# First layer: self_feat of six batches from seven half-size products, token sums on ScalarE, one load and some key products at other places

## The chip, the cores and the metric

The kernel runs on one core of one Trainium2 chip. The core has a matrix engine (TensorE, PE in the profile), a vector engine (VectorE, DVE), an engine for activation functions (ScalarE, ACT), a general engine (GpSimd, POOL) and one that here issues DMA transfers (SyncE, SP). Each works through its own list of instructions in order; semaphores make one wait for another. Matrix products land in PSUM, everything else lies in SBUF. GpSimd does not touch PSUM here.

The metric is the device time of one execution in microseconds, the median of the runs. The profile is one further execution, with the start and end of every instruction.

## The reference

Two layers run on x of shape (8, 512, 512): eight batches, 512 tokens, 512 features. All is float32. Cut to what matters:

```python
# layer 1: attention over the first NONGT = 20 tokens, edges as mask and bias
row_zero  = v.sum(-1) == 0
q_exp     = where(row_zero[..., None], 0, q[:, None, :])
self_feat = concat([v, q_exp], -1) @ W_self.T + b_self
output    = self_feat
for d in range(2):                       # the adjacency and its transpose
    A = (adj if d == 0 else swap(adj))[:, :, :20, :]       # int labels 0/1, last axis 11
    aff = q_heads(self_feat) . k_heads(self_feat[:, :20]) / sqrt(32)     # 16 heads
    aff = where(A.sum(-1) > 0, aff, NEG) + (A @ w_bias + b_bias)
    output += project(softmax(aff) @ self_feat[:, :20]) + bout
x = v + relu(output)

# layer 2: self attention with a layer norm conditioned on q, before and after
h   = gamma(q) * norm(x) + beta(q)
q, k, v = split(h @ Wqkv.T + bqkv)       # 16 heads
out = (softmax(q k^T) / sqrt(512)) @ v
h1  = out @ Wp.T + bp + x
y   = gamma(q) * norm(h1) + beta(q) + h1
```

The part that changes is `self_feat`. Its first 512 input features are x itself, so per batch it is a product of a 512 x 512 weight with a 512 x 512 input. The other 512 are the same condition vector for every live token, which the kernel adds as a bias times a row of ones (`LIVE`); a token whose features sum to zero gets no condition.

## The kernel before, in words

**Layout.** 128 partitions hold one slice of an axis at a time. `VT[b]` is batch b with features on partitions (four slices of 128 by 512 tokens), `ws` the weight, `SF[b]` the result with output features on partitions, `X[b]` the batch with tokens on partitions, `KQ[b]` the keys already multiplied into the query weights. Matrix products accumulate over the four slices.

**Blocks.** The first layer runs over 32 blocks, one per batch b and 128 tokens c (line 565); n is the number of the block, 4 b + c. Three chains of work overlap:

- two blocks ahead, `scores0` (L463): sixteen 320-column matmuls (L471), the query bias added by DVE (L475), then on POOL a multiplication with the mask (L477) and the addition of the edges (L481, in `add_edges`). `less_top` (L484) takes the maximum on DVE (L488) and subtracts it on POOL (L489).
- one block ahead, `normalize0` (L491): the exponential on ACT (L492), the sums and reciprocals on DVE (L495, L496), the division on POOL (L497).
- for the block itself, `turn_weights` (L499): five transposes on PE (L503) and their copy `wt` by ACT (L505), and `result0` (L508): transposes of `SF` (L513) and five matmuls (L515) into PSUM, added to x by DVE (L516), stored to `mid` by SP (L517).

**Work for later batches** lies in the same blocks. `self_feat` (L310) makes a quarter of a later batch's output features: four 512-column matmuls (L300), a bias row by ACT (L307), the addition by DVE (L308). Batch b + 1 gets its last two quarters in blocks c = 0 and 1, and batch b + 2 its first two in c = 2 and 3. `edges` (L242) turns a quarter of the labels into mask and addend, five instructions on DVE (L251 to L255); after the fourth quarter `far_away` (L257) adds the large negative numbers on POOL (L260, L261). At the end of c = 0, `live_sums` (L278) sums X[b + 2] over features on DVE (L281) and compares with zero (L283); in c = 1, `live_of` (L285) transposes that into a row of ones and zeros with PE (L289) and ACT (L291). Loads of X, VT, labels and the value weights for later batches are issued by SP at fixed blocks.

**Keys.** The products of keys and query weights for batches 4 to 7 are made in blocks 10 to 13 (`keys`, L407), half of each before `result0` and half at the end of the block, after the edges (L621). Blocks 15 to 18 also take layer norm statistics of batch 0 (L93), blocks 22 and 23 normalise it (L111).

**Order.** `manual_schedule` keeps the order in which the Python code issues instructions, engine by engine. What waits for what follows from the tiles. A pool with `bufs=4` hands out four buffers in turn; a fifth tile waits until the first one's readers are done. `bank` has four PSUM banks, `pair` two pairs of banks.

**The start.** SP issues the weights, VT of batch 0, `wc`, X of batch 0, `x_kv` (the first 20 tokens of all batches) and further weights. DVE sums `x_kv` (L347) for the condition of the near tokens (PE transposes, L355), and X of batch 0 in `live_sums(0)` (L349). `psk` (L325) occupies both PSUM pairs until DVE has moved it on (L363); the pair of `live_of(0)` comes after.

**The second layer** already makes its q, k, v and output projections of later batches from seven products of half the rows and columns (`product`, L709, matmuls at L719; sums of weights at L685 on DVE, of tokens at L693 on POOL). It is not touched but for a helper, `quarter`, that moves to the top.

Of the kernel before, what the change touches and what calls it, by code (L numbers as in the profile page):

```python
# [18 lines left out]
B, N, F = 8, 512, 512  # L19
P = 128  # L20
C = N // P
# [23 lines left out]
def graph_then_self_attention(ctx: ExitStack, tc: tile.TileContext, x, x_t, near, near_t, labels, w_self_t, wq, wk_t,  # L45
                              wout_t, wg_t, wb_t, wqkv_t, wp_t, cols, gate_vecs, rows, out):
    nc = tc.nc
# [111 lines left out]
    def value(c):  # L159
# [4 lines left out]
            nc.scalar.copy(V[0][:, c, :], out)  # L164
        return Group(f"pv1_0_{c}", lambda k: HT[0][:, k, c * P:(c + 1) * P], lambda k: W1[2][:, k, :], after)


    with ExitStack() as l0:
        w0 = l0.enter_context(tc.tile_pool(name="w0", bufs=1))
# [8 lines left out]
        def bank(name):  # L178
            return ps.tile([P, 512], F32, tag="bank", name=name)
# [34 lines left out]
        load_vt(0)  # L214
        wc = weight("wc", w_self_t[F:2 * F, :])
        x_kv = wring.tile([MH, 2, F], F32, tag="w", name="x_kv")
        load_x(0)
        nc.sync.dma_start(x_kv, near.rearrange("i m f -> m i f"))

        def room(name):  # L220
            return w0.tile([P, 3 * C * HM], F32, tag="kq3", name=name)
# [53 lines left out]

        LT = {}

        def live_sums(b):  # L278

            sums = two.tile([P, C, 1], F32, tag="sums", name=f"sums_{b}")  # L280
            nc.vector.tensor_reduce(sums, X[b], AX.X, ALU.add)  # L281
            LT[b] = two.tile([P, C], F32, tag="lt", name=f"lt_{b}")
            nc.vector.tensor_scalar(LT[b], sums.rearrange("p c o -> p (c o)"), 0.0, None, ALU.not_equal)  # L283

        def live_of(b):  # L285

# [23 lines left out]
        def self_feat(b, blocks_of_f):  # L310

            self_feat_rest(b, self_feat_main(b, blocks_of_f))

        def q_row(b):
            QR[b] = two.tile([P, HM], F32, tag="q_row", name=f"q_row_{b}")
# [249 lines left out]
        for n, (b, c) in enumerate(slots):  # L565
            turn_weights(b, c)

            if n + 3 == len(slots):
                scores0(*slots[n + 2])
            if n + 1 < len(slots):  # L570
                normalize0(*slots[n + 1])
            if n + 3 < len(slots):
                scores0(*slots[n + 2])
            if n + 2 < len(slots):
                add_edges(*slots[n + 2], nc.vector if n + 3 == len(slots) else nc.gpsimd)
            if b + 1 + c // 2 < B:
                self_feat(b + 1 + c // 2, ((c + 2) % 4,))
            if 26 <= n < len(slots) - 2:
                less_top(*slots[n + 2])
            if c == 1 and b + 2 < B:  # L580
                live_of(b + 2)
                if b + 3 < B:
                    load_vt(b + 3)
            if n in (10, 11, 12, 13):
                keys(1, n - 10, 0)
            if n in (24, 25):
                for f in (2 * (n - 24), 2 * (n - 24) + 1):
                    turn(0, f)
            group = {26: lambda: q_or_k(0, 0), 27: lambda: q_or_k(1, 0), 29: lambda: value(0), 30: lambda: value(1),
                     31: lambda: value(2)}.get(n, lambda: None)()  # L590
            if group:
                group.half(0)
                if n < 30:
                    group.half(1)
            if n == 10:
                gate_columns(gb)
            result0(b, c)
            if n >= 30:
                group.half(1)
            if n < 26:  # L600
                less_top(*slots[n + 2])
            if b + 1 + c // 2 < B:
                edges(b + 1 + c // 2, (c + 2) % 4)
            if c == 0 and b + 2 < B:
                live_sums(b + 2)
            if c == 1:
                if b + 1 < B:
                    far_away(b + 1)
                    load_vo(b + 1)
                if b + 2 < B:  # L610
                    load_labels(b + 2)
            if c == 2 and b + 2 < B:
# [51 lines left out]

    M = F // 2
    SUMS = {}

    def quarter(t, p, q):  # L670

        return t[:, 2 * p:2 * p + 2, M * q:M * (q + 1)]

    def a_(i, p, q):
        return quarter(W1[i], q, p)
# [458 lines left out]
```

## Time and profile before

| what | value |
|---|---|
| median of 3 runs | 1322.12 us (1321.79 to 1322.92) |
| profiled execution | 1322.61 us |
| its span, first to last instruction | 1320.8 us |
| mean granted TensorE clock | 0.999 |
| PE busy | 1303.7 us, 99% |
| DVE busy | 945.8 us, 72% |
| POOL busy | 811.3 us, 61% |
| ACT busy | 685.9 us, 52% |
| first transposes (L503) of block 0, block 26, block 31 | 77.51, 356.96, 398.43 us |

A row of a timeline gives start and length in us, engine, line and operation, the tiles written and read, the shape, and in brackets how long the engine had been idle and what ended that. The row of an engine in a list of waits gives the total in us, the count and the longest one. PE is shown twice, as matmuls (PE) and as weight loads (PEld). A float32 matmul or weight load appears as two records. Matmul records overlap[...]: eight records of four 512-column matmuls cover 3.60 us in all, while the last of them is 0.59 us long. So the distance between starts, and not the busy share, tells what a matmul costs.

### The profile page before, as it was taken

To read this page: it belongs to the slowest core of one execution; us is meant where nothing else is said; L and a number is where in the kernel's file an instruction comes from. 1 tells how busy PE (TensorE), PEld (TensorE's weight loads), DVE (VectorE), ACT (ScalarE), POOL (GpSimd) and SP (SyncE) were. 2 spreads that over 40 slices of the span, in tenths; PEclk is the share of its full clock that TensorE was granted. 3 is DMA by queue.
4 is the path that set the end of the run, shared out by engine and by line. 5 is a ranking of instruction groups with operands and counts; after the bars stand their busy time and mean duration, and the time that the engine had idled before them with its cause. 6 is when DMAs were issued, how large, how long until landed. Compare 5 with 4: busy or idle time off the path is not lost.

```text
span 1320.8 us, 29329 instructions
## 1 busy us (share of the span) xinstructions
PE 1303.7 (99%) x11203; PEld 959.1 (73%) x11203; DVE 945.8 (72%) x1721; ACT 685.9 (52%) x1670; POOL 811.3 (61%) x897
## 2 busy tenths in 40 slices
PE   9999999999999999999999999999999999999997
PEld 6566676666665687777777777777777777777776
DVE  4467776677746568687768768776785976776887
ACT  1322222222325666666665666666667567566664
POOL 0056554556563546677577667757866774775776
PEclk9999999999999999999999999999999999999999
DMA  9524552353212000001002000100200010010010
GB/s 337 185 88 138 173 192 74 104 168 127 90 66 72 1 2 1 1 18 65 2 2 81 2 2 17 66 2 1 81 1 1 18 65 1 1 50 2 10 42 33
DMA packets 46490, 78.64 MB, mean 60 GB/s; under 512 B 9680, under 2 KB 14224, under 8 KB 46352
## 3 DMA queue, kind: packets, MB, share of 16 engines
q1 hardware_dynamic: 45920, 76.22, 16.9%
q8 instruction: 90, 1.47, 0.5%
q10 hardware_dynamic: 432, 0.55, 0.1%
q14 instruction: 48, 0.39, 0.1%
HBM read 59.27 MB, written 17.49 MB: 58 GB/s over the span
## 4 chain that ended last, share of the span: by engine, by line
PE 87%; DVE 7%; POOL 2%; issue 1%; DMA 1%; ACT 1%; POOLq 0%; SPq 0%; DVEq 0%; ACTq 0%
PE pst L719 19%; PE pt L875 17%; PE s L850 10%; PE pss L471 9%; PE pao L890 8%; PE psf L300 6%; PE psp L762 6%; PE po L515 2%; PE pqk L138 2%; DVE top L857 2%; PE pz L124 1%; PE ptw L503 1%; PE pw L440 1%; PE pq L421 1%; PE pv L138 1%
## 5 line engine op out<-in xcount | busy, mean ns | idle before, releaser
L870 POOL TENSOR_SCALAR e<-e,den 128x512 f32<-128x512 f32 x511 | 366.8, 718 | 262.4 <-DVE den L867 168.3
L862 ACT ACTIVATE e<-s,top 128x512 f32<-128x512 f32 x512 | 348.9, 699 | 132.0 <-DVE top L857 128.7
L857 DVE TENSOR_REDUCE top<-s 128x2 f32<-128x1024 f32 x256 | 301.0, 1217 | 18.5 <-PE s L850 17.1
L875 PEld LDWEIGHTS pt<-ident,e 128*128 128x128 f32 x2048 | 234.5, 141 | 82.5 <-POOL e L870 25.9
L875 PE MATMUL pt<-ident,e 128*128 128x128 f32 x2048 | 289.7, 276 | 3.4 <-ACT et L877 1.6
L877 ACT COPY et<-pt 128x512 f32<-128x512 f32 x369 | 209.8, 597 | 100.6 <-PE pt L875 99.9
L471 PE MATMUL pss<-kq,sf 128*128 128x320 f32 x512 | 143.2, 433 | 1.0 <-DVE kq L428 1.0
L850 PE MATMUL s<-k_pair,q_pair 32*128 32x512 f32 x992 | 143.7, 640 | 0.0
L890 PEld LDWEIGHTS pao<-et,v 128*32 128x32 f32 x4096 | 107.5, 110 | 44.4 <-issue 44.4
L890 PE MATMUL pao<-et,v 128*32 128x128 f32 x4096 | 126.5, 274 | 0.0
L471 PEld LDWEIGHTS pss<-kq,sf 128*128 128x128 f32 x512 | 94.9, 190 | 37.5 <-ACT sf L307 1.5
L300 PE MATMUL psf<-vt,ws 128*128 128x512 f32 x256 | 115.0, 593 | 0.0
L862 ACT ACTIVATION_READ_ACCUMULATOR e<-s,top 128x1 f32 x512 | 109.4, 214 | 0.0
L877 DVE COPY et<-pt 128x512 f32<-128x512 f32 x143 | 96.3, 673 | 3.4 <-PE pt L875 2.8
L497 POOL TENSOR_TENSOR t<-t,den 128x640 f32<-128x640 f32 x32 | 40.7, 1273 | 81.3 <-DVE den L496 80.7
L300 PEld LDWEIGHTS psf<-vt,ws 128*128 128x128 f32 x256 | 48.3, 190 | 50.7 <-issue 46.6
L505 ACT COPY wt<-ptw 128x640 f32<-128x640 f32 x32 | 22.2, 693 | 104.3 <-PE ptw L503 104.2
L477 POOL TENSOR_TENSOR t<-t,mask 128x640 f32<-128x640 f32 x32 | 49.4, 1544 | 33.8 <-issue 30.2
L489 POOL TENSOR_TENSOR t<-t,top 128x640 f32<-128x640 f32 x32 | 40.7, 1273 | 38.4 <-DVE top L488 38.4
L492 ACT ACTIVATE t<-t 128x640 f32<-128x640 f32 x32 | 23.6, 738 | 77.6 <-POOL t L489 77.6
L126 ACT ACTIVATE ht<-pz,gates_t 128x512 f32<-128x512 f32 x32 | 24.7, 778 | 64.0 <-PE pz L124 64.0
L488 DVE TENSOR_REDUCE top<-t 128x32 f32<-128x640 f32 x32 | 26.2, 818 | 44.3 <-POOL t L481 44.2
(251 smaller groups left out, 2105.9 us busy)
## 6 DMA issues: line engine op xcount, KB each, us to landing
x<-in_x SPq DMA_DIRECT2D x8, 1024.0 KB
mid<-x SPq DMA_DIRECT2D x32, 256.0 KB
xq<-mid SPq DMA_DIRECT2D x8, 1024.0 KB
out<-o SPq DMA_DIRECT2D x31, 256.0 KB
vt<-in_x_t SPq DMA_DIRECT2D x7, 1024.0 KB
labels<-in_labels SPq DMA_DIRECT2D x16, 440.0 KB
wq<-in_wq SPq DMA_DIRECT2D x4, 1024.0 KB
gate<-gates SPq DMA_DIRECT2D x8, 512.0 KB
```

The source lines that it names most:

```text
L300: nc.tensor.matmul(psf[f], ws[:, k, f * P:(f + 1) * P], VT[b][:, k, :], start=(k == 0), stop=(k == C - 1))
L471: nc.tensor.matmul(o, SF[b][:, k, cut], KQ[b][:, k, on], start=(k == 0), stop=(k == C - 1))
L477: nc.gpsimd.tensor_tensor(t, t, MASK[b][:, c, None].to_broadcast([P, H, D2]), ALU.mult)
L719: nc.tensor.matmul(out[:, m, :], fixed[:, k, m * P:(m + 1) * P], moving[:, k, :], start=(k == 0), stop=(k == 1))
L762: nc.tensor.matmul(out[:, m, :], t[:, k, m * P:(m + 1) * P], a[:, k, :], start=(k == 0), stop=(k == 1))
L850: nc.tensor.matmul(S[n][j // 2][:, j % 2, :], Q[b, g][on, c * P:(c + 1) * P], K[b, g][on, :], start=True, stop=True)
L857: nc.vector.tensor_reduce(TOP[n][:, 2 * pair:2 * pair + 2], S[n][pair], AX.X, ALU.max, negate=True)
L862: nc.scalar.activation(e, S[n][pair][:, j % 2, :], AF.Exp, bias=TOP[n][:, j:j + 1], accum_out=DEN[n][:, j:j + 1])
L870: engine.tensor_scalar(E[n][j], E[n][j], DEN[n][:, j:j + 1], att_scale, ALU.mult, ALU.mult)
L875: nc.tensor.transpose(pt[:, k * P:(k + 1) * P], E[n][j][:, k * P:(k + 1) * P], ident)
L877: copy(et, pt.rearrange("p (k n) -> p k n", k=C))
L890: nc.tensor.matmul(PAO[b, g][DH * j:DH * (j + 1), at], V[b][:, k, DH * h:DH * (h + 1)], ET[n, j][:, k, :], start=(k == 0), stop=(k == C - 1))
```

## The change

**Seven products.** For batches 2 to 7, `self_feat` is made in the manner of the second layer: `ws`, `VT[b]` and `SF[b]` are each cut into four quarters (half of the partition slices, half of the columns), and seven products of quarters replace the sixteen full-width matmuls of a batch. One product is two times two matmuls of 256 columns. `weight_sums0` makes four sums of weight quarters once, on DVE, in blocks 0 and 1. `turned_sums` makes four differences of `VT` quarters per batch on POOL: two at the end of block c = 0, one in c = 1, one in c = 2. Products 1 and 2 of batch b + 2 run in c = 2, 6 and 7 in c = 3, then 4 and 5 in c = 0 of the next batch and 3 in c = 1. ACT copies product 1 and writes the four bias rows at once. DVE adds products 2 to 5 from PSUM to the result, and 6 and 7 to a running sum; the running sums (`TO_ADD0`) are added to the result from SBUF by DVE at the end of the block: one addition in c = 2, three in c = 3. Batch 1 keeps the old way.

**Token sums.** `live_sums` uses four ACT copies of X onto itself, one per 128 tokens, each with an accumulated sum, in place of DVE's reduction. It is issued at the same places.

**Places.** `x_kv` is loaded ahead of X of batch 0. The second half of the key products in blocks 10 to 13 is issued ahead of the edges.

```diff
+    M = F // 2
+    def quarter(t, p, q):
+        return t[:, 2 * p:2 * p + 2, M * q:M * (q + 1)]
...
         x_kv = wring.tile([MH, 2, F], F32, tag="w", name="x_kv")
+        nc.sync.dma_start(x_kv, near.rearrange("i m f -> m i f"))
         load_x(0)
-        nc.sync.dma_start(x_kv, near.rearrange("i m f -> m i f"))
...
         def live_sums(b):
-            sums = two.tile([P, C, 1], F32, tag="sums", name=f"sums_{b}")
-            nc.vector.tensor_reduce(sums, X[b], AX.X, ALU.add)
+            sums = two.tile([P, C], F32, tag="sums", name=f"sums_{b}")
+            for c in range(C):
+                nc.scalar.activation(X[b][:, c, :], X[b][:, c, :], AF.Copy, accum_out=sums[:, c:c + 1])
             LT[b] = two.tile([P, C], F32, tag="lt", name=f"lt_{b}")
-            nc.vector.tensor_scalar(LT[b], sums.rearrange("p c o -> p (c o)"), 0.0, None, ALU.not_equal)
+            nc.vector.tensor_scalar(LT[b], sums, 0.0, None, ALU.not_equal)
...
+        parts = l0.enter_context(tc.tile_pool(name="parts", bufs=1))
+        SA, TB, Y0, TO_ADD0 = {}, {}, {}, []
+        def a0(p, q):
+            return quarter(ws, q, p)
+        def weight_sums0(n):
+            SA[n] = a0(1, 0) if n == 2 else parts.tile([P, 2, M], F32, name=f"s{n + 1}_self")
+            x0, x1, how = ((a0(1, 0), a0(1, 1), ALU.add), (SA.get(0), a0(0, 0), ALU.subtract),
+                           (a0(0, 0), a0(1, 0), ALU.subtract), (a0(0, 1), SA.get(1), ALU.subtract))[n]
+            nc.vector.tensor_tensor(SA[n], x0, x1, how)
+        def turned_sums(b, n):
+            B11, B12, B21, B22 = (quarter(VT[b], p, q) for p in range(2) for q in range(2))
+            TB[n] = {0: B12, 3: B21}.get(n) or parts.tile([P, 2, M], F32, tag=f"t{n}", name=f"ts{n + 1}_{b}")
+            x0, x1 = ((B12, B11), (B22, TB.get(0)), (B22, B12), (B21, TB.get(1)))[n]
+            nc.gpsimd.tensor_tensor(TB[n], x0, x1, ALU.subtract)
+        def self_feat_product(b, n):
...
+            o = bank(f"psf_{b}_p{n}").rearrange("p (m n) -> p m n", m=2)
+            for m in range(2):
+                for k in range(2):
+                    nc.tensor.matmul(o[:, m, :], a[:, k, m * P:(m + 1) * P], t[:, k, :], start=(k == 0), stop=(k == 1))
+            if n in (1, 6, 7):
+                less = Y0.get(b)
+                Y0[b] = parts.tile([P, 2, M], F32, tag="y", bufs=2, name=f"ys{n}_{b}")
+                if n == 1:
+                    nc.scalar.copy(Y0[b], o)
+                    for f in range(C):
+                        nc.scalar.activation(SF[b][:, f, :], LIVE[b], AF.Identity, bias=col["b_self"][:, f:f + 1],
+                                             scale=cond_c[:, f, b:b + 1])
+                else:
+                    nc.vector.tensor_tensor(Y0[b], o, less, ALU.add)
+                for p, q in {1: ((0, 0),), 6: ((0, 1),), 7: ((1, 0), (1, 1))}[n]:
+                    TO_ADD0.append((quarter(SF[b], p, q), Y0[b]))
+            for p, q in {2: ((0, 0),), 3: ((0, 1),), 4: ((1, 0),), 5: ((1, 1), (0, 1))}.get(n, ()):
+                nc.vector.tensor_tensor(quarter(SF[b], p, q), o, quarter(SF[b], p, q), ALU.add)
...
-            if b + 1 + c // 2 < B:
-                self_feat(b + 1 + c // 2, ((c + 2) % 4,))
+            if n < 2:
+                self_feat(1, (c + 2,))
+            elif b + 1 + c // 2 < B:
+                for i in ((4, 5), (3,), (1, 2), (6, 7))[c]:
+                    self_feat_product(b + 1 + c // 2, i)
...
+            if n in (10, 11, 12, 13):
+                keys(1, n - 10, 1)
             if b + 1 + c // 2 < B:
                 edges(b + 1 + c // 2, (c + 2) % 4)
...
-            if n in (10, 11, 12, 13):
-                keys(1, n - 10, 1)
+            if n < 2:
+                for i in ((0, 1), (3, 2))[n]:
+                    weight_sums0(i)
+            if b + 2 < B:
+                for i in ((2, 0), (1,), (3,), ())[c]:
+                    turned_sums(b + 2, i)
+            for sf, y in TO_ADD0:
+                nc.vector.tensor_tensor(sf, y, sf, ALU.add)
+            TO_ADD0.clear()
```

More of the change, by code (lines that the diff above doesn't have):

```diff
@@ new lines, in turned_sums @@
+        def turned_sums(b, n):
[5 more added lines that the diff above has]
+            if n == 1:
+                pool, tag = (feat, "feat") if b % 3 == 2 else (feat01, f"feat{b % 3}")
+                SF[b] = pool.tile([P, C, N], F32, tag=tag, name=f"sf_{b}")
+            a = {1: lambda: a0(0, 0), 2: lambda: a0(0, 1), 3: lambda: SA[3], 4: lambda: a0(1, 1), 5: lambda: SA[0],
+                 6: lambda: SA[1], 7: lambda: SA[2]}[n]()
+            t = {1: lambda: quarter(VT[b], 0, 0), 2: lambda: quarter(VT[b], 1, 0), 3: lambda: quarter(VT[b], 1, 1),
+                 4: lambda: TB[3], 5: lambda: TB[0], 6: lambda: TB[1], 7: lambda: TB[2]}[n]()
+            o = bank(f"psf_{b}_p{n}").rearrange("p (m n) -> p m n", m=2)
[5 more added lines that the diff above has]
+                Y0[b] = parts.tile([P, 2, M], F32, tag="y", bufs=2, name=f"ys{n}_{b}")
+                if n == 1:
+                    nc.scalar.copy(Y0[b], o)
[8 more added lines that the diff above has]
+                nc.vector.tensor_tensor(quarter(SF[b], p, q), o, quarter(SF[b], p, q), ALU.add)
@@ L661, in graph_then_self_attention @@
     hp = ctx.enter_context(tc.tile_pool(name="hp", bufs=1, reuse_waits="tile"))
-    M = F // 2
     SUMS = {}
-    def quarter(t, p, q):
-        return t[:, 2 * p:2 * p + 2, M * q:M * (q + 1)]
     def a_(i, p, q):
```

## The prediction

> **What bounds the kernel now.** I read the page first, then the waits of the first layer (90 to 354 us), then its timeline engine by engine, then the starts of every POOL L497 and of the first L503 transpose of each block.
>
> ```profile
> PE 1303.7 (99%) x11203; PEld 959.1 (73%) x11203; DVE 945.8 (72%) x1721; ACT 685.9 (52%) x1670; POOL 811.3 (61%) x897
> ```
>
> TensorE looks like the only bound. But the timeline shows a second one. First the POOL rows that prepare block 7 (batch 1, c = 3), then DVE's in the same stretch:
>
> ```profile
> 136.95 1.56 POOL L477 TENSOR_TENSOR t<-t,mask 128x640 f32<-128x640 f32 x1
> 138.59 1.54 POOL L481 TENSOR_TENSOR t<-t,add 128x640 f32<-128x640 f32 x1
> 141.06 1.27 POOL L489 TENSOR_TENSOR t<-t,top 128x640 f32<-128x640 f32 x1 [0.93 <-DVE top L488]
> ...
> 145.07 1.27 POOL L497 TENSOR_TENSOR t<-t,den 128x640 f32<-128x640 f32 x1 [0.58 <-DVE den L496]
> ```
>
> ```profile
> 140.16 0.82 DVE L488 TENSOR_REDUCE top<-t 128x32 f32<-128x640 f32 x1 [1.83 <-POOL t L481]
> 140.90 0.60 DVE L251 TENSOR_REDUCE total<-labels 128x40 f32<-128x440 int32 x1
> 141.53 0.84 DVE L252 TENSOR_SCALAR mask<-total 128x40 f32<-128x40 f32 x1
> 142.29 0.60 DVE L253 TENSOR_TENSOR labels<-labels,vec 128x440 f32<-128x440 int32 x1
> 142.93 0.61 DVE L254 TENSOR_REDUCE total<-labels 128x40 f32<-128x440 f32 x1
> 143.57 0.24 DVE L255 TENSOR_SCALAR add<-total,vec 128x40 f32<-128x40 f32 x1
> 143.73 0.81 DVE L495 TENSOR_REDUCE den<-t 128x32 f32<-128x640 f32 x1
> 144.57 0.35 DVE L496 RECIPROCAL den<-den 128x32 f32<-128x32 f32 x1
> ```
>
> This is a closed loop. POOL is in order: normalisation of one block (L497), mask and add of the next (L477, L481); then DVE's top, the edges (L251 to L255), den and reciprocal, then L497 of the next block. Each row starts as the one before it ends, and none waits for TensorE. L497 starts at 135.72 and 145.07: 9.35 us a block. Where DVE's token sums lie in the loop (L281, 2.28 us, start to start 2.31) it is 11.75 (123.97 to 135.72). A batch takes 3 x 9.35 + 11.75 = 39.8 us.
>
> TensorE's own block is 9.84 us (L503 at 107.47, 117.31, 127.15), and 10.28 where four `pl` transposes are added: 3 x 9.84 + 10.28 = 39.8. The two bounds are equal. The loop already wins where layer norm statistics (0.99 us of DVE) are added, blocks 18 to 22; TensorE waits:
>
> ```profile
> 274.04 0.76 PE L503 MATMUL ptw<-ident,t 128*128 128x128 f32 x5 [0.50 <-POOL t L497]
> ```
>
> [...] L252 takes 0.84 us under L489 and ends with it, and 0.18 at 30.29 with POOL idle; and this DVE add with two SBUF inputs took 1.88, its own 0.7 after L497's 1.27:
>
> ```profile
> 390.71 1.88 DVE L481 TENSOR_TENSOR t<-t,add 128x640 f32<-128x640 f32 x1 [0.61 <-POOL t L477]
> ```
>
> **The change, part by part.**
>
> *TensorE.* Per batch 16 matmuls of 512 columns become 28 of 256. Eight L300 records (4 matmuls) take 3.42 us at 0.427 us spacing; eight L719 records (the second layer's products of this very shape) 1.71. So 16 x 0.854 = 13.67 against 28 x 0.427 = 11.96: 1.71 less a batch. The blocks c = 2, 3, 0 get two products (3.42, as now); only c = 1, with one, falls from 10.28 to 8.57. Six batches: 10.3 us, if nothing else bounds. TensorE would then need 38.1 a batch. Weight loads of 0.19 stay under a 0.213 spacing.
>
> *DVE, product adds.* Evictions from PSUM lie between L475 and L488, where DVE waits for POOL's mask and add: 3.9 us are free there, and at most three adds of 0.62 (start to start) and L516 (0.61) need 2.5. Cost nothing; if they were late, each would cost 0.62 in the loop. In c = 2 ScalarE first copies product 1 (0.6) and writes four rows of bias (0.73 each); from 6.7 us into the block the first two rows are there at 8.8, and the add of product 2, itself done at 8.5, then still comes ahead of L516 (9.9). Price without that cover: up to 1.4 once a batch.
>
> *DVE, gathered adds* (`TO_ADD0`). These stand after the edges and before the next den, in the loop: one in c = 2, three in c = 3. The row is L685, 0.67 us (0.62 start to start): 0.62 and 1.86.
>
> *Token sums to ScalarE.* DVE loses 2.31 in c = 0. ScalarE gets four copies with accumulation. No such row exists: I take L307's 0.73 start to start plus L862's read of the accumulator, 0.21: 0.95 each, 3.8 in all (bounds 3.2 to 4). Queued behind them are `wt` (L505) and the next exp. x is issued at 120.24 and its last packets land at 125.1; the sums would run to about 129, wt was due at 127.95 and its reader L515 runs at 136: hidden. DVE's `lt` comes at 132: no wait.
>
> *POOL token differences.* Four subtractions of 128x512, 1.28 each (L693, same shapes): two after c = 0, one after c = 1, one after c = 2, each right behind L489, just where DVE does the edges. Here the lock decides. Times are from the start of L488. L489 ends at 2.17; L252, waiting, runs then; L253 (two SBUF inputs) and the subtraction now compete.
> - c = 0: if L253 goes first it ends at 2.7, the first subtraction at 4.0, L255 waits for it, the second ends at 5.4, and `lt` waits for that: den starts at 5.5. If the subtraction goes first: 3.5, L253 4.1, second subtraction 5.4, L255 after it: 5.5 as well. Now it is 3.57. +1.95.
> - c = 2: den at 4.75 or 5.5 with the gathered add; middle +1.55.
> - c = 1: `far` (L260, L261) waits for L252 and L255 and ends at 4.3; the subtraction ends at 5.6, where L497 would start at 4.95: +0.75.
> - c = 3: no subtraction, the three adds: +1.86.
>
> So the loop is 11.3 + 10.1 + 10.9 + 11.2 = 43.5 us a batch against 39.8. The one-time weight sums (four adds of 0.67) add 1.3 in block 0 and 0.8 in block 1.
>
> The subtractions' inputs don't wait: `vt` of batch b + 2 is issued three blocks ahead (135.64, for a use near 160 us), and the one that overwrites a quarter waits for a product of its own block, done by then. The next `vt` load on SP waits for the last product in c = 1, as it does for L300 now.
>
> *Loads and keys.* `x_kv` ahead of `x_0`: TensorE's 1.20 us wait at 18.63 goes, but its next stop is a PSUM pair that DVE frees at 22.59 behind `lt`, and `lt` now waits for ScalarE: x_0 lands about 17.0, plus 3.8 is 20.8, as now (20.71). Nothing; bounds -1.2 and +1. Key copies ahead of the edges: same DVE work, in blocks where TensorE is slower (13.1 us).
>
> **The sum.** L497 of block 1 starts at 84.19. Loop steps of blocks 0 to 8: 12.55, 10.9, 10.9, 11.2, 11.3, 10.1, 10.9, 11.2, 12.4 (1.1 for the gate vectors, as now) = 101.45, so 185.6; 1.3 later block 10's transposes start: 187.0 against 179.27, +7.7. Blocks 10 to 13 (keys) are TensorE's: 53.0 - 1.71, so 238.3 against 232.28, +6.0. Blocks 14 and 15 are TensorE's too: L497 of block 16 at 256.6. Then 12.2, 12.3, 11.1, 11.9 (statistics), 11.2, 11.3, 10.1, 11.8, 12.1 (normalisation, 0.9), 9.35 = 113.3: 369.9, transposes 371.2 against 356.96, +14.3. From there TensorE's 9.84 is longer than the loop's 9.35, and the second layer is unchanged: the delay stays. 1320.8 + 14.3 = 1335.1 of span, 1.8 around it (1322.61 - 1320.8), and the profiled execution is 0.5 over the median: **1336.4 us**.
>
> **Rivals.**
> - *Part of the lock.* If the small L255 and `lt` don't take it, c = 0 is 9.8 and c = 2 10.4: 41.5 a batch, about +5: 1327. For it: the one-element L96 shows no delay under POOL (0.153).
> - *No conflict* (the subtractions run beside the edges): gathered adds 2.5 + `lt` 0.1 + 0.75 in c = 1: 40.7; losses early and in blocks 19 to 25 and the 1.71 saved in the key blocks cancel: 1322, no change. Against it: the rows above.
> - *Faster.* TensorE stays the bound and 6 x 1.71 = 10.3 is kept: 1312. That needs the loop at 38.1 or less, extras of at most 38.1 - 37.4 = 0.7 us a batch; the gathered adds alone are 2.5, so they would have to run while DVE waits for POOL (its idle time before L488: 27.9 us in the list of waits, 90 to 354 us). The order puts them before den.
> - *Worse.* ScalarE waits for a late x and holds wt and exp, or the subtractions win every time: 1342 and more.
>
> **How the numbers follow.** Forecast (1330 to 1341) 0.55, part of the lock 0.20, no conflict 0.13, faster 0.07, worse 0.05. A measurement here can tell about 0.2% (2.6 us) from no change. Slower 0.80, same 0.13, faster 0.07. The range 1323 to 1341 leaves out "faster", "worse" and the lower half of "no conflict": about 0.19.
>
> **What would show it.** Right: L497 starts about 11.3, 10.1, 10.9, 11.2 us apart instead of 11.75, 9.35, 9.35, 9.35; TensorE idle before `ptw`, put down to POOL, in most blocks from 2 to 10 and 17 to 25; L253 or L255 stretched from 0.60 and 0.24 by about 1 us under the subtractions. Wrong: `ptw` at 8.57 in c = 1 without waits (the loop doesn't bind), edges at their present lengths (no lock), or ScalarE idle before its sums with `wt` late.

## The result and the profile after

| | before | changed |
|---|---|---|
| median | 1322.85 us (11 runs, 1321.68 to 1323.43) | 1327.02 us (11 runs, 1323.85 to 1328.58) |
| ratio | 1 | 1.003, 95% interval 1.002 to 1.0039 |
| profiled execution, its span | 1322.61, 1320.8 us | 1324.78, 1323.0 us |
| first transposes of blocks 0, 10, 14, 26, 31 | 77.51, 179.27, 232.28, 356.96, 398.43 us | 77.03, 181.61, 233.31, 358.83, 401.09 us |

The changed kernel is slower by 4 us, where I had forecast 14. The same kernel run again (e4 below) had a median of 1325.47, so the loss is 3 to 4 us; the changed kernel's times spread over 4 to 5 us, and the profiled execution lies at the low end of them. Lines have moved: division L497 is now L555, mask L535, edge addition L539, top L546, its subtraction L547, the edges L257 to L261, den L553, reciprocal L554, `ptw` L561; the new lines are L290 (sums on ScalarE), L342 (token differences), L370 (product additions), L692 (gathered additions).

The page's line of busy time of the changed kernel:

```profile
PE 1298.1 (98%) x11347; PEld 988.7 (75%) x11347; DVE 958.4 (72%) x1759; ACT 708.8 (54%) x1740; POOL 841.5 (64%) x921
```

TensorE has lost 5.6 us of work and the kernel is longer: it waits. The list of waits of the changed kernel from 90 to 400 us (engine, what waits, for what; total us, times, longest):

```profile
PE ptw L561 <- POOL t L555: 9.6, 11, 2.0
```

Before, the same row read 1.4 us, 4 times. From the timeline of PE, the transposes of block 18, which waited 0.50 us before:

```profile
273.92 0.77 PE L561 MATMUL ptw<-ident,t 128*128 128x128 f32 x5 [1.26 <-POOL t L555]
```

The second bound does decide. Its steps for batch 1, from one L555 to the next, against those of the forecast:

| edges of block | before | forecast | changed |
|---|---|---|---|
| c = 2 | 9.35 | 10.9 | 10.18 |
| c = 3 | 9.35 | 11.2 | 11.14 |
| c = 0 | 11.75 | 11.3 | 9.66 |
| c = 1 | 9.35 | 10.1 | 9.94 |
| batch | 39.8 | 43.5 | 40.9 |

TensorE follows these steps: the transposes of blocks 3 to 7 start 10.18, 11.13, 9.66 and 9.95 us apart. Two steps are as forecast; c = 0 and c = 2 are not. First c = 1, which prepares block 7 as the rows shown of before did. The changed kernel's timeline of POOL, then of DVE:

```profile
142.81 1.27 POOL L547 TENSOR_TENSOR t<-t,top 128x640 f32<-128x640 f32 x1 [0.93 <-DVE top L546]
144.21 1.04 POOL L266 TENSOR_SCALAR far<-mask 128x160 f32<-128x160 f32 x1
145.72 0.53 POOL L267 TENSOR_TENSOR add<-add,far 128x160 f32<-128x160 f32 x1 [0.47 <-DVE add L261]
146.21 1.27 POOL L342 TENSOR_TENSOR ts<-vt 128x512 f32<-128x512 f32 x1
147.44 1.27 POOL L555 TENSOR_TENSOR t<-t,den 128x640 f32<-128x640 f32 x1
```

```profile
141.91 0.82 DVE L546 TENSOR_REDUCE top<-t 128x32 f32<-128x640 f32 x1 [2.62 <-POOL t L539]
...
145.48 0.81 DVE L553 TENSOR_REDUCE den<-t 128x32 f32<-128x640 f32 x1
146.33 0.35 DVE L554 RECIPROCAL den<-den 128x32 f32<-128x32 f32 x1
```

DVE is done at 146.68, as early as ever (den 3.57 us after the top). POOL isn't: the difference stands ahead of the division, which starts as it ends. Here POOL itself is the chain.

Now c = 0, where the forecast had den 5.5 us after the top. The timeline of POOL and of DVE of the changed kernel, batch 1:

```profile
133.16 1.27 POOL L547 TENSOR_TENSOR t<-t,top 128x640 f32<-128x640 f32 x1 [0.93 <-DVE top L546]
134.40 1.73 POOL L342 TENSOR_TENSOR ts<-vt 128x512 f32<-128x512 f32 x1
136.20 1.27 POOL L342 TENSOR_TENSOR vt<-vt 128x512 f32<-128x512 f32 x1
137.50 1.27 POOL L555 TENSOR_TENSOR t<-t,den 128x640 f32<-128x640 f32 x1
```

```profile
132.27 0.82 DVE L546 TENSOR_REDUCE top<-t 128x32 f32<-128x640 f32 x1 [1.45 <-POOL t L539]
...
134.40 0.60 DVE L259 TENSOR_TENSOR labels<-labels,vec 128x440 f32<-128x440 int32 x1
135.03 0.61 DVE L260 TENSOR_REDUCE total<-labels 128x40 f32<-128x440 f32 x1
135.68 0.49 DVE L261 TENSOR_SCALAR add<-total,vec 128x40 f32<-128x40 f32 x1
136.09 0.16 DVE L292 TENSOR_SCALAR lt<-sums 128x4 f32<-128x4 f32 x1
136.16 0.81 DVE L553 TENSOR_REDUCE den<-t 128x32 f32<-128x640 f32 x1
137.00 0.35 DVE L554 RECIPROCAL den<-den 128x32 f32<-128x32 f32 x1
```

By the lock I mean what the prediction's rows of L252 and L481 show: a DVE and a POOL instruction of which one lasts longer while the other is at work (L252 0.84 us under L489, 0.18 with POOL idle). That the other pairs priced there would do so was my estimate. The rows here agree with it. The first difference takes 1.73 us, not 1.27, beside L259, which keeps its 0.60 and so seems to have gone first; L261 takes 0.49, not 0.24, and ends with the difference. But `lt` runs at 136.09, ahead of the second difference at 136.20, and waits for nothing. So den starts 3.89 us after the top instead of 5.5, and the second difference runs beside den. Both chains end together: the reciprocal reaches POOL 0.5 us after its start (137.00), and POOL's second difference ends at 136.20 + 1.27, where the division starts.

One more row differs from what I had priced, ScalarE's sums (timeline of ACT, changed kernel):

```profile
167.56 0.63 ACT L290 ACTIVATE x<-x 128x512 f32<-128x512 f32 x1 [2.57 <-DVE sf L692]
168.09 0.18 ACT L290 ACTIVATION_READ_ACCUMULATOR x<-x 128x1 f32 x1
168.19 0.61 ACT L290 ACTIVATE x<-x 128x512 f32<-128x512 f32 x1
```

A sum comes every 0.61 to 0.63 us, the reading of the accumulator included; four take about 2.5 us, not 3.8.

### The profile page after: what moved, and what is told of

Its sections match the earlier page's. It is cut to its first block, busy times and chain, and to the rows that moved or that the text cites. A ratio compares the mean times of both kernels' runs of the same rounds, so it can differ in the third digit from the quotient of the medians.

```text
span 1323.0 us, 29745 instructions
## 1 busy us (share of the span) xinstructions
PE 1298.1 (98%) x11347; PEld 988.7 (75%) x11347; DVE 958.4 (72%) x1759; ACT 708.8 (54%) x1740; POOL 841.5 (64%) x921
## 4 chain that ended last, share of the span: by engine, by line
PE 74%; DVE 13%; POOL 8%; issue 3%; ACT 1%; DMA 0%; POOLq 0%; DVEq 0%; ACTq 0%
PE pst L786 18%; PE pt L942 16%; PE s L917 9%; PE pao L957 8%; PE psp L829 6%; PE pss L529 3%; POOL t L535 3%; POOL t L539 3%; PE psf_p L356 2%; PE pqk L138 1%; DVE top L924 1%; DVE top L546 1%; DVE mask L258 1%; PE pz L124 1%; DVE den L553 1%
## 5 line engine op out<-in xcount | busy, mean ns | idle before, releaser
L937 POOL TENSOR_SCALAR e<-e,den 128x512 f32<-128x512 f32 x511 | 361.8, 708 | 267.1 <-DVE den L934 172.7
L555 POOL TENSOR_TENSOR t<-t,den 128x640 f32<-128x640 f32 x32 | 40.7, 1272 | 59.6 <-DVE den L554 54.0
L535 POOL TENSOR_TENSOR t<-t,mask 128x640 f32<-128x640 f32 x32 | 49.4, 1544 | 31.2 <-issue 30.3
L546 DVE TENSOR_REDUCE top<-t 128x32 f32<-128x640 f32 x32 | 26.2, 818 | 56.3 <-POOL t L539 56.3
L547 POOL TENSOR_TENSOR t<-t,top 128x640 f32<-128x640 f32 x32 | 40.7, 1271 | 34.0 <-DVE top L546 34.0
L917 PEld LDWEIGHTS s<-k_pair,q_pair 32*128 32x128 f32 x992 | 41.0, 183 | 20.8 <-issue 17.3
L786 PE MATMUL pst<-t,w 128*128 128x256 f32 x224 | 53.7, 383 | 0.0
```

The lines of the kernel that those rows point to most:

```text
L535: nc.gpsimd.tensor_tensor(t, t, MASK[b][:, c, None].to_broadcast([P, H, D2]), ALU.mult)
L547: nc.gpsimd.tensor_tensor(tv, tv, top.to_broadcast([P, 2 * H, NG]), ALU.subtract)
L786: nc.tensor.matmul(out[:, m, :], fixed[:, k, m * P:(m + 1) * P], moving[:, k, :], start=(k == 0), stop=(k == 1))
L917: nc.tensor.matmul(S[n][j // 2][:, j % 2, :], Q[b, g][on, c * P:(c + 1) * P], K[b, g][on, :], start=True, stop=True)
L937: engine.tensor_scalar(E[n][j], E[n][j], DEN[n][:, j:j + 1], att_scale, ALU.mult, ALU.mult)
```

## The experiments

The theory is that of the prediction, with the measured steps: whatever stands between top and division, on DVE or POOL, sets the time in the first layer. The main rival is that place does not matter, only the amount of work and locking.

**e1: the gathered additions in the gap.** The prediction's rival "faster" asked for the additions to run while DVE waits for POOL's mask and edge addition. Here up to 2, 1 and 1 of them are put off to blocks c = 0, 1 and 3, ahead of the product additions.

```diff
+                for sf, y in TO_ADD0[:(2, 1, 0, 1)[c]]:
+                    nc.vector.tensor_tensor(sf, y, sf, ALU.add)
+                del TO_ADD0[:(2, 1, 0, 1)[c]]
                 for i in ((4, 5), (3,), (1, 2), (6, 7))[c]:
...
-            for sf, y in TO_ADD0:
-                nc.vector.tensor_tensor(sf, y, sf, ALU.add)
-            TO_ADD0.clear()
```

> The changed kernel with the gathered additions (TO_ADD0) issued one block later, ahead of the product additions, where DVE waits for POOL's mask and add; everything else as in the changed kernel. Theory 'loop' (POOL division, mask, add, DVE top, edges, gathered additions, den, reciprocal, division is the bound): the loop loses 4 x 0.62 = 2.5 us a batch, from 40.9 to about 38.5, TensorE needs 38.1 a batch, so nearly all of the intended gain appears: 1316 to 1318, ratio to the kernel before about 0.996. Rival 'engine load' (it is DVE's total of work that counts): the same additions, so as the changed kernel, 1324 to 1328. Rival 'late evictions' (PSUM banks held by additions that come later): slower than the changed kernel, over 1328.

Measured: 1327.94 us, ratio to before 1.0037 (1.0025 to 1.005). A miss: the theory had 1316 to 1318, and the rival that counts only the amount of work 1324 to 1328. What decides between them is the trace. The timeline of DVE, then of POOL, of this kernel (the additions are L638):

```profile
126.32 3.26 DVE L638 TENSOR_TENSOR sf<-ys,sf 128x512 f32<-128x512 f32 x2
129.69 1.89 DVE L370 TENSOR_TENSOR sf<-psf_p,sf 128x512 f32<-128x512 f32 x3
131.49 0.68 DVE L574 SCALAR_TENSOR_TENSOR x<-po,x 128x512 f32<-128x512 f32 x1
132.09 0.81 DVE L546 TENSOR_REDUCE top<-t 128x32 f32<-128x640 f32 x1
```

```profile
127.04 2.00 POOL L535 TENSOR_TENSOR t<-t,mask 128x640 f32<-128x640 f32 x1
129.12 1.88 POOL L539 TENSOR_TENSOR t<-t,add 128x640 f32<-128x640 f32 x1
```

The gap is open because POOL is at work, and it was no free place for these DVE additions with two SBUF inputs. Two of them take 3.26 us instead of about 1.3, and POOL's mask and addition take 2.00 and 1.88 beside DVE's additions, not 1.54. Here the top at 132.09 no longer waits for POOL but follows DVE's own queue. Steps, in the order of the table: 9.58, 9.79, 11.49, 10.39, together 41.25: what c = 2 and c = 3 gained, c = 0 and c = 1 gave back. My expectation left these waits out, and so did the rival "faster" of the prediction.

**e2: no token differences.**

```diff
-            TB[n] = {0: B12, 3: B21}.get(n) or parts.tile([P, 2, M], F32, tag=f"t{n}", name=f"ts{n + 1}_{b}")
-            x0, x1 = ((B12, B11), (B22, TB.get(0)), (B22, B12), (B21, TB.get(1)))[n]
-            nc.gpsimd.tensor_tensor(TB[n], x0, x1, ALU.subtract)
+            TB[n] = (B12, B22, B22, B21)[n]
```

> The changed kernel without the four token differences per batch on POOL: the products read the undiminished quarters of VT, so these products are of other numbers, and nothing waits for a difference. [...] the loop falls by what the differences cost in it, 0.3 (c = 0), 0.6 (c = 1), 0.2 (c = 2), together about 1.0 of 40.9 us a batch; over the five batches that the loop bounds 4 to 5 us less than the changed kernel: about 1321 to 1322. The larger price of the prediction (3.5 a batch) would give 12 us or more: 1314. Rival 'the differences cost nothing': as the changed kernel, 1324 to 1328.

Measured: 1320.43 us, ratio 0.998 (0.9973 to 0.9987), a little below the theory's 1321 to 1322 and far from the 1314 that the prediction's price would give. Steps 9.94, 11.15, 9.41, 9.33: the differences cost 0.2, 0, 0.25 and 0.6 us, 1.1 a batch, not the 4.25 of the forecast (1.55 + 1.95 + 0.75, of which 0.62 in c = 2 is the gathered addition's; 3.6 without it).

**e3: the sums and the places alone.** The kernel before with only the token sums and both places of the change.

```diff
-            nc.vector.tensor_reduce(sums, X[b], AX.X, ALU.add)
+            for c in range(C):
+                nc.scalar.activation(X[b][:, c, :], X[b][:, c, :], AF.Copy, accum_out=sums[:, c:c + 1])
...
```

> The kernel before with only the token sums on ScalarE and the two changed places; self_feat of all batches as before, no seven products. Theory 'loop': its step after c = 0 falls from 11.75 to about 9.45, the loop to 37.5 us a batch, TensorE's 39.8 is the bound everywhere and the waits in blocks 18 to 24 go: 2 to 4 us faster than before, 1319 to 1321. Rival 'ScalarE holds wt or x is late for it': slower than before. Rival 'places cost': slower than before by up to 2.

Measured: 1319.28 us, ratio 0.9972 (0.9962 to 0.9982), in the theory's interval and faster than both kernels. No `ptw` waits for POOL from 90 to 354 us, and from 240 to 400 us PE is busy 160.00 of 160 us. This part of the change is a gain of 3.5 us; the seven products then lose it, and as much again.

**e4: the changed kernel once more.** No edit.

> The changed kernel once more, for a second profile and the spread of its time: runs lay between 1323.9 and 1328.6, in two heaps near 1324 and 1327, while those of the kernel before lay within 1.8 us. If the heaps come from loads that land at other times, a trace of the upper heap shows ScalarE's sums waiting longer for x and the blocks after them later; if they come from the granted clock, the same blocks with a lower clock.

Measured: 1325.47 us (18 runs), ratio 1.0022 (1.0015 to 1.0029). Where the two heaps of times come from, its trace doesn't tell: it is that of a short execution (1324.99 us). The clocks of the single executions follow with e11 and e12.

**e5: no gathered additions.**

```diff
-            for sf, y in TO_ADD0:
-                nc.vector.tensor_tensor(sf, y, sf, ALU.add)
```

> The changed kernel without the four gathered additions of each batch (the parts of self_feat that they would bring are left out, so the output is other numbers). Theory 'the second bound': the additions are 0.62 us of block c = 2 and 1.86 us of block c = 3 on the chain ahead of the division, so the loop falls from 40.9 to about 38.4 us per batch, as TensorE's 38.1: about 2.5 us x 5.75 batches = 14 us less than the changed kernel, 1310 to 1314 us. Rival 'it is the whole traffic, not the place' (the loss is spread over the lock and the other new instructions): no more than 4 us less, 1321 to 1324 us.

Measured: 1313.61 us, ratio 0.9933 (0.9921 to 0.9946), in the theory's interval. Steps 9.58, 9.34, 9.68, 9.94: c = 2 and c = 3 lose 0.60 and 1.80 us, the rest nothing. Its DVE timeline in c = 3, where three additions had stood between these rows:

```profile
123.91 0.24 DVE L261 TENSOR_SCALAR add<-total,vec 128x40 f32<-128x40 f32 x1
124.07 0.81 DVE L553 TENSOR_REDUCE den<-t 128x32 f32<-128x640 f32 x1
```

24 short additions, 15 us of DVE, cost 12 to 13 us of the kernel's time (1325.5 to 1327 against 1313.6).

**e6: the sums on DVE again.**

```diff
-            for c in range(C):
-                nc.scalar.activation(X[b][:, c, :], X[b][:, c, :], AF.Copy, accum_out=sums[:, c:c + 1])
+            nc.vector.tensor_reduce(sums, X[b], AX.X, ALU.add)
...
```

> The changed kernel with the token sums as one reduction of 2.3 us on VectorE again, all else as changed. Theory 'the second bound': the sums lie in block c = 0, on the chain ahead of the division, six times: +2.3 us x 6 = +13 us, about 1337 to 1340 us. Rival 'the sums were under cover of TensorE': 1325 to 1329 us, as the changed kernel.

Measured: 1336.97 us, ratio 1.0104 (1.009 to 1.0117). That is the lower edge of the theory's interval. Step c = 0 is 11.97 us, the others stay. The DVE timeline of c = 0:

```profile
137.77 0.49 DVE L261 TENSOR_SCALAR add<-total,vec 128x40 f32<-128x40 f32 x1
138.17 2.27 DVE L289 TENSOR_REDUCE sums<-x 128x4 f32<-128x2048 f32 x1
140.48 0.17 DVE L291 TENSOR_SCALAR lt<-sums 128x4 f32<-128x4 f32 x1
```

That this time equals my forecast for the changed kernel is chance.

**e7: both places put back.**

```diff
-        nc.sync.dma_start(x_kv, near.rearrange("i m f -> m i f"))
         load_x(0)
+        nc.sync.dma_start(x_kv, near.rearrange("i m f -> m i f"))
...
-            if n in (10, 11, 12, 13):
-                keys(1, n - 10, 1)
             if b + 1 + c // 2 < B:
                 edges(b + 1 + c // 2, (c + 2) % 4)
...
+            if n in (10, 11, 12, 13):
+                keys(1, n - 10, 1)
```

> The changed kernel with the load of x_kv after that of x_0 and the key products' second half after the edges, as before. My theory gave both places nothing: 1325 to 1328 us; the load alone is worth +0.5 us by the two traces (first block 77.03 against 77.51 us). If the key products' place matters, the four blocks 10 to 13 change their length by over 0.5 us each and the time by 2 us or more.

Measured: 1327.13 us, ratio 1.0033 (1.002 to 1.0045): not to be told from the changed kernel by the times. The load: block 0 begins at 76.67 us here, and anywhere from 76.17 to 78.75 in the other kernels that have the change's order; the 0.48 us between the two first traces is no effect. The key products: blocks 11, 12 and 13 keep their length within 0.02 us. But block 14 takes 11.17 us, in the changed kernel 9.92, by a wait that the kernel before has too (PE timeline of this kernel):

```profile
237.77 2.93 PE L529 MATMUL pss<-kq,sf 128*128 128x320 f32 x10 [1.00 <-DVE kq L486]
```

The scores of batch 4 need the last key copies, which DVE made after the edges. The new place takes this wait away: 1.2 us, where the forecast gave nothing.

Block 10 is 1.4 us longer here than in the changed kernel, for another reason. From the windows of 2 us of this kernel (engines' busy us and counts, granted clock, DMA share, GB/s):

```profile
182.00:184.00 2.00, 2.00 (x6) 1.41 (x5) 0.00 (x0) 0.69 (x1) 1.92 (x2) 0.50 0.57 203
```

TensorE has just waited for POOL (its transposes start at 181.28, after 1.99 us idle), and from 182 to 185 us its granted clock is 0.50. e1 shows the same at the same place, the changed kernel's profiled execution and e4's, with a wait of 1.97 us there, do not. e11 and e12 follow this up.

**e8: a reduction put under the lock.** L258, the mask, waits about 0.65 us in most blocks for POOL's subtraction of the top (0.84 us, where the same instruction before, L252, took 0.18 with POOL idle). The second reduction of the edges (0.61 us) is put off to the next block and placed there, ahead of the mask; c = 1 puts nothing off.

```diff
...
             nc.vector.tensor_reduce(total, src, AX.X, ALU.add)
+            late = LATE.pop() if LATE else None
+            if late:
+                nc.vector.tensor_reduce(late[0], late[1], AX.X, ALU.add)
             nc.vector.tensor_scalar(MASK[b][:, c, :], total, 0.0, None, ALU.is_gt)
             nc.vector.tensor_tensor(weighted, src, edge_bc[:, None, 0:L].to_broadcast([P, D2, L]), ALU.mult)
+            if late:
+                nc.vector.tensor_scalar(late[2], late[0], edge_bc[:, L:L + 1], None, ALU.add)
+            if defer:
+                LATE.append((total, weighted, ADD[b][:, c, :]))
+                return
             nc.vector.tensor_reduce(total, weighted, AX.X, ALU.add)
...
-                edges(b + 1 + c // 2, (c + 2) % 4)
+                edges(b + 1 + c // 2, (c + 2) % 4, c != 1)
```

> The changed kernel with the second reduction of the edges (0.61 us) and their last addition put off to the next block, in blocks c = 0, 2, 3; there the reduction stands between the first reduction and the mask, which waits 0.7 us for GpSimd's subtraction of the top. Theory 'the second bound': about 0.65 to 0.85 us less ahead of the division in three of four blocks, 1.9 to 2.5 us per batch, about 38.4 to 39.0 for the loop: 11 to 14 us less than the changed kernel, 1311 to 1316 us, below both kernels. Rival 'the bound is TensorE and a clock': 1325 to 1328 us.

Measured: 1321.05 us, ratio 0.9987 (0.998 to 0.9994). Right in sign, but outside the expected 1311 to 1316: a third to a half of the size. Steps 10.10, 10.37, 9.65, 10.04: only c = 3 gained (0.77). In c = 0 POOL's two differences set the step, as shown above. In c = 2 the removed reduction had been the cover of a difference. DVE's timeline of this kernel, then POOL's:

```profile
113.56 0.60 DVE L264 TENSOR_TENSOR labels<-labels,vec 128x440 f32<-128x440 int32 x1
114.09 1.76 DVE L702 TENSOR_TENSOR sf<-ys,sf 128x512 f32<-128x512 f32 x1
115.77 0.81 DVE L563 TENSOR_REDUCE den<-t 128x32 f32<-128x640 f32 x1
```

```profile
113.56 1.74 POOL L352 TENSOR_TENSOR vt<-vt,ts 128x512 f32<-128x512 f32 x1
```

The gathered addition now comes 0.6 us earlier, into the difference, and takes 1.76 us in place of 0.68: den starts 4.34 us after its top (111.43), 4.42 in the changed kernel.

One more pair of rows of this kernel bears on the prediction. In block 0 the deferred reduction brings `lt` (L302 here) to its place earlier, when the first difference is already at work. DVE's timeline, then POOL's:

```profile
91.29 1.24 DVE L302 TENSOR_SCALAR lt<-sums 128x4 f32<-128x4 f32 x1
```

```profile
90.76 1.74 POOL L352 TENSOR_TENSOR ts<-vt 128x512 f32<-128x512 f32 x1
```

Here `lt` takes 1.24 us instead of 0.16 and ends with the difference. So `lt` does wait for a difference that is already at work; in the changed kernel it came before the second difference.

**e9: the first product straight from PSUM.** Product 1 is added to its quarter by a DVE instruction with one SBUF input, in the gap, where e1 had put instructions with two.

```diff
-                for p, q in {1: ((0, 0),), 6: ((0, 1),), 7: ((1, 0), (1, 1))}[n]:
+                for p, q in {1: (), 6: ((0, 1),), 7: ((1, 0), (1, 1))}[n]:
                     TO_ADD0.append((quarter(SF[b], p, q), Y0[b]))
-            for p, q in {2: ((0, 0),), 3: ((0, 1),), 4: ((1, 0),), 5: ((1, 1), (0, 1))}.get(n, ()):
+            for p, q in {1: ((0, 0),), 2: ((0, 0),), 3: ((0, 1),), 4: ((1, 0),), 5: ((1, 1), (0, 1))}.get(n, ()):
```

> The changed kernel with one edit: the first product is added to its quarter of self_feat straight from PSUM, in the gap of block c = 2, in place of the gathered addition of its copy (the copy stays, for the other sums). Theory 'the place ahead of the division': block c = 2 loses 0.6 us (10.18 to about 9.6), 6 x 0.6 = 3.6 us less than the changed kernel: 1320.5 to 1323.5 us. Rival 'the additions cost the same wherever they stand': 1325 to 1328 us.

Measured: 1322.64 us, ratio 0.9999 (0.9991 to 1.0008): the changed kernel's loss is gone, with as many additions as before. Step c = 2 is 9.58 (10.18 in the changed kernel), the others as they were. In the gap DVE's timeline, then POOL's, are now

```profile
108.24 1.47 DVE L370 TENSOR_TENSOR sf<-psf_p,sf 128x512 f32<-128x512 f32 x2
```

```profile
108.95 1.55 POOL L535 TENSOR_TENSOR t<-t,mask 128x640 f32<-128x640 f32 x1
```

POOL's mask keeps its 1.55 us, where e1 had 2.00. The edit changes the place and the source at once. But at the old place the addition took only its own 0.68 us in the changed kernel (114.76 us), so it was the place that cost, and the source that made the new place free.

**e10: e8 and e9 together.**

> e8 (the second reduction of the edges put off) and e9 together. In e8 the gathered addition of block c = 2 waited 1.1 us for GpSimd's token difference (1.76 us in place of 0.68), so that block kept its 10.1 us. Theory 'lock': without that addition block c = 2 falls to about 9.4 us, c = 3 stays at 10.4, c = 0 and c = 1 at GpSimd's own chain of 9.65 and 10.0 us: 39.4 per batch against 40.2 in e8, 6 x 0.7 = 4 us less than e8's 1321.1: 1316 to 1318.5 us, below both kernels. Rival 'another wait takes its place': 1320 to 1322 us.

Measured: 1316.94 us, ratio 0.9953 (0.994 to 0.9965): 6 us below the kernel before, 8 to 10 below the changed one. Steps 8.76, 10.38, 9.66, 10.04, 38.8 a batch. In c = 2 DVE's and POOL's timelines are now

```profile
112.27 0.60 DVE L264 TENSOR_TENSOR labels<-labels,vec 128x440 f32<-128x440 int32 x1
113.11 0.82 DVE L563 TENSOR_REDUCE den<-t 128x32 f32<-128x640 f32 x1 [0.24 <-ACT t L560]
```

```profile
112.27 1.74 POOL L352 TENSOR_TENSOR vt<-vt,ts 128x512 f32<-128x512 f32 x1
114.47 1.28 POOL L565 TENSOR_TENSOR t<-t,den 128x640 f32<-128x640 f32 x1 [0.46 <-DVE den L564]
```

The difference still waits for L264, but nothing waits for the difference, and den waits for the exponential. I had expected 9.4 us for this step; at 8.76 den waits for the exponential alone, and no longer for the edges.

**e11 and e12: the wait of block 10 filled.** In e11 TensorE gets four more matmuls of 512 columns at the end of block 9, in e12 two; nobody reads their result.

```diff
+            if n == 9:
+                fill = bank("fill")
+                for k in range(C):
+                    nc.tensor.matmul(fill, ws[:, k, 0:P], VT[b + 1][:, k, :], start=(k == 0), stop=(k == C - 1))
             for sf, y in TO_ADD0:
```

> The changed kernel with four matmuls of 512 columns more on TensorE, whose result nobody reads, at the end of block 9, where TensorE waits 1.97 us for the division of block 10 (they last 1.7 us and make nothing late). In two kernels (e1 and e7) the granted clock fell to 0.50 for 3.4 us right after this wait, in the changed kernel's own profiled executions it did not. Theory 'the wait brings the clock down in some executions': the times of 1326 to 1329 us become rare and the median falls to 1324 to 1325 us. Rival 'the spread has another cause': the same spread as the changed kernel, 1324 to 1328.5 us, median 1325.5 to 1327 us.

Measured: 1325.55 us (9 runs, 1325.16 to 1327.76), ratio 1.0025 (1.0015 to 1.0035); 3 of 9 times above 1326 us. The size of the fill was my mistake: four such matmuls take 3.4 us, as the forecast itself had counted them. The transposes come without a wait, at 182.55, about 1.3 us late.

> As e11, with two matmuls in place of four: in e11 the four lasted 3.4 us and made block 10 1.3 us late. Two last 1.7 us, less than the wait of 1.97. Theory 'the wait brings the clock down in some executions': block 10 is not late, the median is 1324 to 1325 us and at most one time in five is over 1326 us (13 of 29 were, 8 of 11 and 5 of 18, in the changed kernel's two series). Rival 'the spread has another cause': a median of 1325.5 to 1327 us, over a third of the times above 1326 us.

Measured: 1325.15 us (21 runs, 1324.33 to 1327.54), ratio 1.002 (1.0013 to 1.0026); the wait is 0.25 us. 5 of 21 times are above 1326 us. My count in the expectation was wrong: in the changed kernel's two series it was 15 of 29, 8 of 11 and 7 of 18. So long times became rarer, as the theory says, but not as rare as it asked for, and the two series of the changed kernel differ among themselves by more. The median of e11 lies in the rival's interval, that of e12 in neither.

The mean granted clock of each execution says more. It was 0.998 in 11 of the 15 executions of the changed kernel above 1326 us and in 2 of the 14 below, but in only 1 of the 30 of e11 and e12. That speaks for a lower clock after the wait as one cause of the long times. It is not shown: no long execution of the changed kernel was traced, the series ran on different chips, and 7 of the 8 long times of e11 and e12 come without a lower clock.

## Why the prediction was right or wrong

**The bound: right.** The closed loop over POOL's division, not TensorE, decides: `ptw` waits for it, and e5, e6 and e9, which change what stands ahead of den, move the time by most of what they move the steps: -12 to -13 us (by the steps of six batches about -14), +10 to +11.5 (+14), -3 to -4 (-3.6). Of the forecast's signs, TensorE's waits before `ptw` came in 10 of the 18 blocks named.

**The gathered additions: right.** 0.62 and 1.86 forecast, 0.60 and 1.80 by e5.

**The sums: right for DVE** (2.31 forecast, 2.31 by e6's step). Their price on ScalarE was too high, 3.8 against about 2.5 us; hidden in both.

**The token differences: here the forecast failed.** The step is "`lt` waits for that: den starts at 5.5 ... +1.95" in c = 0. The lock is there and L259, the first difference and L261 go in the order and at the times of my first alternative, within 0.2 us. But `lt` ran ahead of the second difference, so den started 3.89 us after the top, beside that difference. That made 11.3 into 9.66, 1.64 us in batch 1, and as much in batches 4 and 5. In c = 2 I took the middle of two values, +1.55; L259 went first, as in the lower of the two (+1.18), and since L261 ends with the difference and doesn't run after it, the step was only +0.83. In c = 1 +0.75 was forecast and +0.59 measured. The sign that I had named, L253 or L255 (now L259 and L261) longer by about 1 us, didn't come: L259 kept 0.60 us, L261 went from 0.24 to 0.49. All four differences cost 1.1 us a batch (e2), where 3.6 was forecast. The four steps together are 40.9 instead of 43.5.

**"Nothing" for the places: half wrong.** The key copies' old place held up the scores of block 14 by 1.0 us (e7), a wait that the forecast left out.

**The sum, point by point.** Against the forecast, the span is 12.1 us shorter (1323.0 for 1335.1). Up to block 10 it is 5.4 (181.61 for 187.0); in blocks 10 to 13, 0.4 is lost (51.7 for 51.3); from block 14 to 26 it is 7.4 (125.5 for 132.9), 1.2 of it by the key copies; after block 26 0.3 is lost (block 28 takes 7.08 us, 6.40 before, and the transposes after it wait 0.51 us for POOL). Per batch the four steps are 2.6 us below the forecast, 2.4 of them in c = 0 and c = 2.

**The rivals.** "Part of the lock", with 41.5 a batch and 1327 us, comes nearest to the numbers: 9.8 and 10.4 us for c = 0 and c = 2, where 9.66 and 10.18 were measured. I gave it 0.20. But its reason is not what happened. It supposed that L255 and `lt` don't take the lock, because the one-element L96 shows no delay. L261 did wait (0.49 us), and so does `lt` where it comes late (1.24 us in e8); what saved the time was the order. That its number fits is in part luck. "Faster" named the gap as the place that would save the change; e1 shows that it isn't for additions from SBUF (3.26 us for two, POOL's mask 2.00), and e9 that it is for one from PSUM (1.47 for it and the product addition behind it, the mask 1.55).

## What to carry to other kernels

Where instructions of two engines wait for each other, as DVE's and POOL's did here, their order counts as well as their lengths; here one short instruction (`lt`, 0.16 us) ahead of a long one (the second difference, 1.27 us) instead of behind it, as forecast, was 1.6 us a batch. Work out both orders, take the one that a trace shows, and don't average. A gap that one of these engines leaves because the other is at work was free in these runs for additions with one input from PSUM (e9, POOL's mask at 1.55 us), and not for those with two from SBUF (e1, the mask at 2.00). And before an instruction is moved off the critical chain, look at what it covered there: e8's gain was half eaten by a wait that the moved reduction had hidden.

## What the runs showed of the hardware that I had not expected

- **Who goes first.** In the changed kernel and in e8 the rows read as if the waiting DVE instruction ran after a POOL instruction, the next one of DVE too, and only then POOL's next: L258 and L259 (0.60 us, its usual length), then the first difference (1.73 us instead of 1.27); L261, then (`lt` at 136.09) the second at 136.20; in e8 L263 and L264 (0.60 us), then the difference (1.74 us), for which L702 waited (1.76 us). There the waiting instruction was short and ended within 0.05 us of POOL's. DVE doesn't get two turns every time: in e1 the division ended at 127.08, POOL's mask took from 127.04 to 129.04, and the second of the two additions ended 0.54 us after the mask. What decides the order, the runs don't show.
- **The lock costs both.** In e1 DVE's additions lengthened POOL's mask and addition from 1.54 to 2.00 and 1.88 us, and two of the additions took 3.26 us instead of about 1.3.
- **Small does not mean free.** A `tensor_scalar` of 128x4 waited for a difference in e8 (1.24 us, 0.16 alone), as L261 of 128x40 did (0.49 us, 0.24 alone); L96 of 128x1 did not: it takes 0.15 us in every one of its 63 records of the kernel before, that inside POOL's L809 (588.28 us) among them.
- **The edges' reduction took no longer beside POOL.** L260 takes 0.61 us beside a difference (changed kernel, 135.03 us) and with POOL idle (123.89 us), and 0.60 in e8 beside POOL's subtraction.
- **Sums on ScalarE come every 0.61 us** for 128x512, with the 0.18 us of the accumulator's reading inside that distance. A plain copy of this size from PSUM (L361) lasts 0.59 us.
- **A half clock after some of the longest waits.** In the first layer TensorE's clock fell to 0.50 in e1, e6 and e7, for 3.4 us each. These falls began within about 1 us of the end of a wait: of 2.10 us in e1, of 1.99 us in e7, where it cost 1.4 us, and of 2.74 us in e6, whose mean clock of 0.99 from 240 to 400 us leaves room for one more. It stayed at 1.00 after waits of 1.97 us (changed kernel and e4), 1.90 us (e1) and 1.72 us (e9). Between 1.97 and 1.99 us the length of the wait alone can hardly decide; what does, the traces don't show.
